# Selective scan: normed rows scaled by VectorE in place of ScalarE

## The chip, the cores and the metric

The kernel runs on one core of a Trainium2 chip, as one launch. The metric is the device time of an execution in microseconds (us), as the median of several executions. The engines are named as the profile names them: PE is TensorE (PEld its weight loads), DVE is VectorE, ACT is ScalarE, POOL is GpSimd, SP is SyncE. They run beside each other, each through its own instructions in a fixed order, and wait for one another by semaphores.

## What is computed

Four transformer layers on 32 sequences of 256 rows with 128 features, in fp32. Each layer normalises its rows, applies an attention-like part, adds it, normalises again and applies a feed-forward part. Only the first half of layer 0 bears on the change:

```python
h = _layernorm(x) * (1 + ca) + sa            # first norm, with per-sequence scale and shift
x = x + ga * attn(h)                         # attn: the part below

def attn(h):                                 # in outline
    n = _layernorm(h) * ln_w + ln_b          # second norm
    p = n @ proj_W.T + proj_b ; z = silu(p)
    for br in (forward, backward):
        u = softplus(p @ conv_W[br].T + conv_b[br])
        dbc = u @ deltaBC_W.T                # delta (64), B (16), C (16)
        delta = softplus(dbc[:, :64] @ dt_W.T + dt_b)
        # per feature d and state n (16 states), along the 256 rows of a sequence:
        #   hs[t] = exp(delta[t] * A[d, n]) * hs[t-1] + delta[t] * u[t] * B[t, n]
        #   y[t]  = sum over n of hs[t] * C[t, n] ; y += u * D
    return (y_forward + y_backward) * z + h

def _layernorm(x):
    return (x - mean(x)) / sqrt(var(x) + 1e-5)   # over the 128 features of a row
```

## The kernel before

The 8192 rows are cut into 16 batches of 512 (two sequences). `x[b]` stays in SBUF with features on partitions and rows along the free axis. The eight half layers run as eight stages, one after another; the change lies in the first, `scan_layer`.

A batch of the scan has 2 branches x 16 states = 32 recurrences along 512 rows. They are taken in 8 groups of four states, p = 8b to 8b + 7. For a group:

- PE multiplies `duT` with `Bd` into the PSUM tile `dB` (16 products of 32 rows; the tile has one buffer). `Bd` is the B of a branch spread out into a diagonal, made by POOL in four multiplications (`scan_b`, line 916).
- DVE runs four scans (`TENSOR_TENSOR_SCAN hs<-decay,dB`, line 953), one for each state, with the factors `decay` that ACT has made by Exp (`scan_decay`; a ring of 10 buffers).
- PE transposes the result in two halves into `hT` (one buffer), ACT copies each to `hsT`, and PE multiplies these with `Cd` into `y`, which collects the whole batch.

The scan of a group may start when its `dB` is complete, and the next `dB` may be written when the last of the four scans has read this one. The instructions are recorded in an order written out by hand: an agenda of steps, two for each group (2p and 2p + 1); PE, DVE, ACT and POOL keep that order. A batch has T = 16b as its first step, and what prepares batch b is put at steps before T, so it runs among the scans of batches b - 1 to b - 3; what prepares the first ones runs ahead of the first scan.

Each batch needs two norms (n = 1, starting at step o = T - 44, from `x`; n = 2, at o = T - 36, from `h`). A norm goes through these steps:

- o: `norm_rows`: four PE transposes give rows on partitions; ACT copies them from PSUM to `ln_xn` (four tiles of 128 rows, 128x512 together, one buffer).
- o + 1: `norm_sums`: DVE takes mean and variance (four `bn_stats` to `ln_st`, four `bn_aggr` to `ln_mv`); POOL adds the eps (`ln_v`).
- o + 2: `scan_roots`: ACT makes exp(-0.5 ln v) (`ln_t`, `ln_rs`); POOL refines it by a Newton step in four small instructions (`norm_newton`, lines 527 to 530, the last one writing `ln_rs`) and makes the shift -mean * root in two more (`ln_m`).
- o + 3, behind the work of that step: `norm_scale`: ACT scales `ln_xn` in place, four instructions of 128x128 with scale `ln_rs` and bias `ln_m`.
- o + 4: `norm_out`: PE transposes the four tiles back, ACT applies the factor and shift of the features (`h` or `xn`).

Of the eight groups of a batch, the fourth (p % 8 == 3) is the one whose odd step holds a scaling for n = 1, and the last (p % 8 == 7) that for n = 2. In the order of DVE the place after these steps' work lies between the four scans of that group and the four of the next. On POOL the newton steps are followed directly by the four `Bd` multiplications of a branch, at both places. `Bd` waits for ACT's copy `bc` (line 912).

The instructions of `norm_scale` have line 428 in the profile, where `act` records them; most of the others have line 320, of a wrapper that keeps the order, so the tiles' names tell them apart. PE's are at 416 (products) and 425 (transposes).

Of the kernel before, what the change touches and what calls it, by code (L numbers as in the profile page):

```python
# [25 lines left out]
ALU = mybir.AluOpType  # L26
# [312 lines left out]
class Program:  # L339
# [372 lines left out]
    def scan_layer(self, w):  # L712
# [7 lines left out]
        with ExitStack() as ctx:  # L720
# [14 lines left out]
            for n in range(10):  # L735
                t = self.wk_pool.tile([P, 2, SEQ], F, name=f"decay{n}", bufs=1)
# [6 lines left out]
            def put(t, f, *args):  # L743
                agenda.setdefault(t, []).append((f, args))
# [11 lines left out]
            behind, scale = {}, {}  # L756
# [7 lines left out]
            for b in range(NB):  # L764
                a = s[b] = {"b": b}
                T = 16 * b
                put(T, self.clear_regions)


                for o, n, src in ((T - 44, 1, lambda a: self.x[a["b"]]), (T - 36, 2, lambda a: a["h"])):  # L770

                    put(o, lambda a, n=n, src=src: a.update({("rows", n): self.norm_rows(src(a), sums=False)}), a)
                    put(o + 1, lambda a, n=n: a.update({("st", n): self.norm_sums(a["rows", n], nc.gpsimd)}), a)
                    put(o + 2, lambda a, n=n: self.scan_roots(a, n), a)
                    scale.setdefault(o + 3, []).append(lambda a=a, n=n: self.norm_scale(a["st", n][0], *a["r", n]))
                put(T - 40, self.scan_norm_out, a)
                put(T - 32, self.scan_norm_out2, s, a)
                put(T - 21, self.scan_proj, s, a)
                put(T - 20, self.scan_gate, s, a)
                put(T - 19, self.scan_gate2, s, a)  # L780
                for br in (0, 1):
                    o = T + 8 * br
                    put(T - 19 + 6 * br, self.scan_u, s, a, br)
                    put(T - 18 + 6 * br, self.scan_u2, s, a, br)
                    put(o - 15, self.scan_delta, s, a, br)
                    put(o - 14, self.scan_rows, s, a, br)
                    put(o - 13, self.scan_chunks, s, a)
                    put(o - 10, self.scan_turn, s, a, br)
                    put(o - 9, self.scan_b, s, a, br)
                    put(o - 5, self.scan_c, s, a, br)  # L790
                put(T - 4, lambda a: nc.gpsimd.tensor_scalar(a["uu"], a["uu"], w.vec[:, 6:7], None, ALU.mult), a)
                put(T + 21, self.scan_end, s, a)

                put(T + 25, lambda a: self.residual(0, 0, a["b"], a["y"]), a)
# [10 lines left out]

    def scan_roots(self, a, n):
        _, mv, v = a["st", n]
        a["r", n] = self.norm_newton(mv, v, self.norm_roots(v))

    def scan_norm_out(self, a):  # L810
        a["h"] = self.norm_out(a["st", 1][0], self.ada_mods(0, 0, a["b"]), "h")
# [2515 lines left out]
```

## Time and profile before

| | |
|---|---|
| time, median of 5 runs (lowest to highest) | 5791.92 us (5789.57 to 5795.16) |
| the profiled execution: its time, its span | 5801.96 us, 5800.2 us |
| mean granted TensorE clock of it | 0.952 |
| share of the span that is busy: PE, DVE, ACT, POOL | 90%, 67%, 63%, 51% |
| first to last scan (all 16 batches) | 120.2 us to 970.4 us of the span |
| scalings of `ln_xn` by ACT at line 428 | 128 instructions, 486 ns median, 23.8 us to 825.3 us |
| the same scaling done by DVE elsewhere in the program, SBUF to SBUF | 120 instructions, 329 / 345 / 793 ns (least, median, most) |
| four of them together | 1.11 us to 2.06 us |
| one `Bd` multiplication on POOL | 1048 ns (1043 to 1057) |

How to read it. The profile is of one execution, which took 10.04 us longer than the median of the runs. A line of the timeline begins with the start and the time from the first start to the last end (us from the start of the span), then engine, line, operation, out<-in with shapes, and how many equal instructions were merged (xN); in brackets stands the idle time of the engine before them and what ended it. Consecutive instructions on an engine overlap a little, so the next one can start before the shown end of the last. A line of the windows gives a stretch and its length, then the busy us and number of instructions of each engine, the clock granted to PE, and the share of the DMA engines.

### The profile page before, as it was taken

To read this page: it belongs to the slowest core of one execution; us is meant where nothing else is said; L and a number is where in the kernel's file an instruction comes from. 1 tells how busy PE (TensorE), PEld (TensorE's weight loads), DVE (VectorE), ACT (ScalarE), POOL (GpSimd) and SP (SyncE) were. 2 spreads that over 40 slices of the span, in tenths; PEclk is the share of its full clock that TensorE was granted. 3 is DMA by queue.
4 is the path that set the end of the run, shared out by engine and by line. 5 is a ranking of instruction groups with operands and counts; after the bars stand their busy time and mean duration, and the time that the engine had idled before them with its cause. 6 is when DMAs were issued, how large, how long until landed. Compare 5 with 4: busy or idle time off the path is not lost. (4 is left out here: it accounts for less than half of the span.)

```text
span 5800.2 us, 159517 instructions
## 1 busy us (share of the span) xinstructions
PE 5238.8 (90%) x66753; PEld 2967.5 (51%) x66753; DVE 3894.2 (67%) x7981; ACT 3643.6 (63%) x5550; POOL 2969.8 (51%) x3597
## 2 busy tenths in 40 slices
PE   5888887879989999999999877999899998999976
PEld 3666665446646666665666443555322222545543
DVE  3888887631156766666665645888778763677778
ACT  4999996223355555555555644666588885777733
POOL 3666663566457777776766334665455552111100
PEclk8999998789999999999999887999999997999988
DMA  2111101124312222222222221110244441000010
GB/s 74 45 36 48 47 34 45 37 73 135 103 53 74 75 74 74 74 74 77 76 71 72 84 37 40 37 34 27 62 97 98 98 97 32 20 23 23 21 41 28
DMA packets 311313, 343.48 MB, mean 59 GB/s; under 512 B 106624, under 2 KB 206208, under 8 KB 310336
## 3 DMA queue, kind: packets, MB, share of 16 engines
q1 hardware_dynamic: 269456, 240.04, 14.9%
q0 software_dynamic: 23920, 58.05, 3.9%
q10 hardware_dynamic: 17216, 35.19, 1.6%
q8 instruction: 524, 8.59, 0.6%
q14 instruction: 197, 1.61, 0.1%
HBM read 139.17 MB, written 122.68 MB: 45 GB/s over the span
## 5 line engine op out<-in xcount | busy, mean ns | idle before, releaser
L320 POOL TENSOR_SCALAR_AFFINE_SELECT E<-E 128x512 f32<-128x512 f32 (+2 forms) x1024 | 795.2, 779 | 674.1 <-ACT E L320 649.9
L320 DVE TENSOR_REDUCE mt<-S 128x4 f32<-128x1024 f32 (+2 forms) x768 | 756.1, 999 | 419.0 <-PE S L416 415.3
L320 ACT ACTIVATE E<-S 128x1024 f32<-128x1024 f32 (+2 forms) x704 | 632.0, 907 | 528.2 <-PE S L416 484.6
L320 DVE TENSOR_TENSOR_SCAN hs<-decay,dB 128x512 f32<-128x512 f32 x512 | 582.9, 1205 | 103.8 <-PE dB L416 81.5
L428 ACT ACTIVATE hid<-S,bigw 128x1024 f32<-128x1024 f32 x512 | 537.9, 1113 | 86.1 <-PE S L416 80.4
L320 DVE TENSOR_TENSOR E<-S,cst 128x1024 f32<-128x1024 f32 x320 | 390.1, 1219 | 195.7 <-PE S L416 182.7
L416 PE MATMUL S<-kx,q 32*128 32x512 f32 (+1 forms) x2048 | 519.6, 598 | 1.9 <-DVE mt L320 1.5
L416 PE MATMUL S<-qa,kx 32*128 32x256 f32 x4096 | 511.3, 372 | 10.6 <-ACT E L320 5.2
L2871 POOL TENSOR_TENSOR acc<-acc,ye 128x512 f32<-128x512 f32 x256 | 346.2, 1352 | 336.6 <-DVE ye L320 324.7
L320 ACT COPY E<-S 128x1024 f32<-128x1024 f32 x320 | 324.3, 1014 | 281.7 <-PE S L416 252.2
L416 PEld LDWEIGHTS S<-qa,kx 32*128 32x128 f32 x4096 | 326.8, 185 | 172.6 <-issue 67.5
L416 PE MATMUL S<-qG,f 32*128 32x512 f32 x2560 | 365.0, 640 | 12.1 <-DVE E L320 12.1
L416 PE MATMUL S<-hm,bigw 32*128 32x512 f32 x2048 | 352.9, 649 | 9.5 <-ACT hid L428 8.3
L428 ACT ACTIVATE decay<-dl,A 128x510 f32<-128x510 f32 x512 | 338.7, 713 | 0.0
L425 PE MATMUL hT<-cst,hs 128*128 128x128 f32 x2048 | 279.6, 280 | 29.5 <-ACT hsT L428 22.7
L428 ACT ACTIVATE hsT<-hT 128x1024 f32<-128x1024 f32 x256 | 260.1, 1016 | 58.2 <-PE hT L425 56.1
L416 PE MATMUL po<-E,vz 128*32 128x256 f32 x4096 | 286.7, 363 | 1.4 <-POOL E L320 1.4
L416 PE MATMUL po<-E,vzl 128*32 128x128 f32 x8192 | 284.9, 274 | 1.3 <-POOL E L320 1.0
L416 PE MATMUL tp<-hid,bigw 128*32 128x512 f32 x2048 | 275.2, 610 | 8.2 <-DVE ye L320 6.9
L416 PE MATMUL tp<-h,w 128*32 128x256 f32 (+1 forms) x2592 | 258.7, 465 | 21.3 <-ACT kx L320 10.0
L416 PEld LDWEIGHTS po<-E,vzl 128*32 128x32 f32 x8192 | 225.0, 110 | 103.3 <-ACT phi_e L320 45.5
L320 DVE TENSOR_TENSOR ye<-tp,gb 128x512 f32<-128x512 f32 x256 | 174.2, 685 | 147.3 <-issue 78.2
(557 smaller groups left out, 11949.2 us busy)
## 6 DMA issues: line engine op xcount, KB each, us to landing
gb<-gT SPq DMA_DIRECT2D x256, 256.0 KB
wide<-oc SPq DMA_DIRECT2D x192, 256.0 KB
regions<-zeros ACTq DMA_DIRECT2D x16, 2048.0 KB
nm<-wide SPq DMA_DIRECT2D x384, 64.0 KB
rb<-far SPq DMA_DIRECT2D x384, 64.0 KB
rx<-far SPq DMA_DIRECT2D x64, 256.0 KB
expert_rows<-eo SPq DMA_DIRECT2D x39, 256.0 KB
bigw<-in_s SPq DMA_DIRECT2D x18, 256.0 KB
```

Of the source, the lines that this page charges most:

```text
L320: made = self.tc.keep_in_program_order(op(*args, **kw))
L416: return self.tc.keep_in_program_order(self.nc.tensor.matmul(out, lhsT, rhs, start=start, stop=stop, **kw))
L425: return self.tc.keep_in_program_order(self.nc.tensor.transpose(out, in_, self.c.ident[:k, :k]))
L428: ins = self.nc.scalar.activation(*args, **kw)
L2871: nc.gpsimd.tensor_tensor(a["acc"], a["acc"], ye, ALU.add)
```

## The change

The four scalings of a norm in the scan stage are recorded for DVE in place of ACT, at the same point of the program: `tensor_scalar` with two operations, subtract the mean, multiply by the root, in place on `ln_xn`. The shift is no longer made, so two small POOL instructions of each norm go. The 16 x 2 norms of the stage are all changed; the other stages are not.

```diff
-                    scale.setdefault(o + 3, []).append(lambda a=a, n=n: self.norm_scale(a["st", n][0], *a["r", n]))
+                    scale.setdefault(o + 3, []).append(lambda a=a, n=n: self.scan_norm_scale(a, n))
...
     def scan_roots(self, a, n):
         _, mv, v = a["st", n]
-        a["r", n] = self.norm_newton(mv, v, self.norm_roots(v))
+        a["r", n], _ = self.norm_newton(mv, v, self.norm_roots(v), False)
+
+    def scan_norm_scale(self, a, n):
+        xn, mv, _ = a["st", n]
+        for t in range(4):
+            self.nc.vector.tensor_scalar(
+                xn[:, t], xn[:, t], mv[:, t, 0:1], a["r", n][:, t : t + 1], ALU.subtract, ALU.mult
+            )
```

In the order of the built programs, ACT has 128 instructions less, POOL 64 less and DVE 128 more; all else stands in the same order on every engine.

## Prediction

> **What bounds it now.** I read the windows by batch first, then the timeline of one steady batch engine by engine (715.10 us to 769.04 us), then every place where DVE does this scaling already.
>
> The windows of two batches of the scan: one with both norms, and the next, which holds nearly no norm work.
>
> ```profile
> core 0: us, PE busy (x) PEld busy (x) DVE busy (x) ACT busy (x) POOL busy (x), PEclk, DMA share, GB/s
> 769.03:822.96 53.93, 47.83 (x700) 33.81 (x700) 46.05 (x60) 51.41 (x86) 35.54 (x44) 1.00 0.12 43
> 822.96:874.84 51.88, 45.17 (x688) 32.35 (x688) 44.22 (x44) 47.55 (x74) 33.03 (x31) 1.00 0.13 45
> ```
>
> A batch takes 53.93 us and ACT is busy for 51.41 of them: the fullest engine, but not alone. Without nearly all norm work the next batch takes 51.88, only 2.05 less though ACT has 3.86 less to do. So the period is a chain through PE, DVE and ACT, and must be followed.
>
> DVE's timeline:
>
> ```profile
> 720.51 0.75 DVE L320 TENSOR_SCALAR dl<-tp,w 128x512 f32<-128x512 f32 x1 [0.86 <-PE tp L416]
> 735.85 4.56 DVE L320 TENSOR_TENSOR_SCAN hs<-decay,dB 128x512 f32<-128x512 f32 x4
> 741.76 4.55 DVE L320 TENSOR_TENSOR_SCAN hs<-decay,dB 128x512 f32<-128x512 f32 x4 [1.36 <-PE dB L416]
> 760.70 0.75 DVE L320 TENSOR_SCALAR u<-tp,w 128x512 f32<-128x512 f32 x1 [0.87 <-PE tp L416]
> 769.04 1.22 DVE L320 TENSOR_TENSOR_SCAN hs<-decay,dB 128x512 f32<-128x512 f32 x1 [1.36 <-PE dB L416]
> ```
>
> At both places of the new scaling (ahead of 741.76 and of 769.04) DVE idles 1.36 us while PE refills `dB`. Four scalings alone take 1.11, so they would fit, if their root is ready and nothing stands in their way. ACT, POOL and PE there:
>
> ```profile
> 740.71 0.26 ACT L428 ACTIVATE bc<-tp 128x128 f32<-128x128 f32 x1
> 742.09 1.65 ACT L428 ACTIVATE ln_xn<-ln_xn,ln_m,ln_rs 128x128 f32<-128x128 f32 x4
> 749.54 1.03 ACT L428 ACTIVATE hsT<-hT 128x1024 f32<-128x1024 f32 x1 [0.64 <-PE hT L425]
> 768.48 0.26 ACT L428 ACTIVATE bc<-tp 128x128 f32<-128x128 f32 x1
> ```
>
> ```profile
> 739.61 0.20 POOL L320 TENSOR_TENSOR ln_rs<-ln_rs,ln_t 128x4 f32<-128x4 f32 x1
> 741.05 4.07 POOL L320 TENSOR_TENSOR Bd<-cst,bc 128x512 f32<-128x512 f32 x4 [0.65 <-ACT bc L428]
> 768.27 0.20 POOL L320 TENSOR_TENSOR ln_rs<-ln_rs,ln_t 128x4 f32<-128x4 f32 x1
> ```
>
> ```profile
> 742.63 1.48 PE L425 MATMUL tp<-cst,ln_xn 128*128 128x128 f32 x4
> 747.25 1.17 PE L416 MATMUL dB<-Bd,duT 32*128 32x128 f32 x32
> ```
>
> POOL starts `Bd`, four pieces of 1.05 us, just when DVE will scale. How the two get on is seen in another stage (merged rows share a start; x2 and x3 are the first two and three of the x4):
>
> ```profile
> 4301.09 1.11 DVE L320 TENSOR_SCALAR ln_xn<-ln_xn,ln_mv,ln_rs 128x128 f32<-128x128 f32 x4
> ...
> 1706.43 2.06 DVE L320 TENSOR_SCALAR ln_xn<-ln_xn,ln_mv,ln_rs 128x128 f32<-128x128 f32 x4
> 1706.43 1.10 DVE L320 TENSOR_SCALAR ln_xn<-ln_xn,ln_mv,ln_rs 128x128 f32<-128x128 f32 x2
> 1706.43 1.81 DVE L320 TENSOR_SCALAR ln_xn<-ln_xn,ln_mv,ln_rs 128x128 f32<-128x128 f32 x3
> 1707.05 0.41 POOL L320 TENSOR_SCALAR_AFFINE_SELECT E<-E 128x256 f32<-128x256 f32 x1
> 1707.43 0.73 POOL L320 TENSOR_TENSOR glob<-glob,lv 128x256 f32<-128x256 f32 x1
> ```
>
> Alone, pieces follow each other by 0.26 and the last ends 0.34 after its start. Beside POOL the second ended at 1707.53, 0.07 after the select's end (1707.46), the third at 1708.24, 0.08 after `glob`'s end (1708.16). I read: a piece needs something it shares with POOL from 0.26 to 0.34 after its start; if a POOL instruction is in it, the piece waits for that one's end, slips through in 0.08, and the next piece meets the next POOL instruction.
>
> When POOL takes it is seen in the same stage:
>
> ```profile
> 758.24 2.50 POOL L320 TENSOR_TENSOR Cd<-cst,bc 128x512 f32<-128x512 f32 x2
> 759.03 0.81 DVE L320 SCALAR_TENSOR_TENSOR sg<-xp,sg 128x512 f32<-128x512 f32 x1
> ```
>
> The second `Cd` starts 1.01 after the first, 759.25, and ends at 760.74: 1.49 instead of 1.05, held for 0.44 until `sg` ended at 759.84. So it wanted the thing about 0.15 after its start.
>
> **The change, part by part.** Removed from ACT: 8 scalings a batch, 2 x 1.54 us of its queue (742.09 to the next start at 743.63). Removed from POOL: two `ln_m` instructions a norm, 0.6 us, so that `Bd` can follow `ln_rs` sooner. Added to DVE: 8 pieces a batch, and a wait for POOL's `ln_rs`; behind it in DVE's queue stand the next four scans.
>
> *Middle scaling.* `ln_rs` is ready at 739.81, the scan of the fourth group ends at 740.4. The pieces start at about 740.33 and want the shared thing at 740.59, 740.85, 741.11 and 741.37. `Bd` starts at 741.05 and wants it at 741.20: three pieces pass, the fourth waits for the first `Bd`, until 742.10. The scans start at 742.10 instead of 741.76: 0.34 lost. What is won: PE's transposes were paced by ACT and ended at 744.11; now all is there when PE comes to them (742.65), and four take 0.60. PE is ready for `dB` at about 746.3 instead of 747.25, but the scans end at 746.24 + 0.34, so `dB` starts at 746.60: 0.65 earlier. ACT, which idled 0.64 at 749.54 for the `hT` behind this `dB`, goes on 0.65 earlier, and works without a gap to the second norm's roots; so all of that comes 0.65 earlier, POOL's newton and `bc` too (the wait of 0.87 at 760.70 shrinks with it).
>
> *Late scaling.* The root is ready at 768.47 - 0.65 = 767.82. The first piece starts at 767.86 and wants the shared thing at 768.12. `bc` ends at 768.09, `Bd` starts 0.08 behind it as before (740.97 to 741.05), 768.17, and wants it at 768.32. One piece passes; the second wants it at 768.38, and from there each waits for one more `Bd`: ends at 769.22, 770.23 and 771.24, and 771.31 for the last piece. The next batch's scans start at 771.24 instead of 769.04: 2.20 lost. Given back: before, the next `dB` came 5.88 us after the scans' start (715.10 to 720.98), since PE was late behind the paced transposes (the wait of 0.86 at 720.51). Now PE has its transposes, products and `hT` done by 774.8 (771.4 plus 0.65, 1.09, 1.02, 0.64), and `dB` starts right behind the scans, 4.48 after their start (741.76 to 746.24): 1.40 won. Net 0.80 lost per batch. From that `dB` on the order of waits is the old one (ACT waits for `hT`, PE for `yT`), so it repeats: 13 of the 16 batches hold both scalings (26 of 32), 13 x 0.80 = 10.4 us lost.
>
> *Ahead of the first scan* lie six scalings in a nearly serial chain. In the first, `ln_rs` ends at 23.20 and ACT scaled from 23.83 to 25.48; DVE alone ends at 24.35, 1.13 won; four such, 4.5 won. At the fifth (`ln_rs` 96.12, `bc` 96.07) `Bd` is free to start at about 96.32 (it came 0.20 behind POOL's last small instruction before), and three pieces wait: 99.47 instead of 98.39, 1.1 lost. At the sixth (122.21) `Bd` can follow the newton at once, so all four wait, to 126.3; and the first scan, which ran from 120.24, stands behind them: the second `dB` comes at 130.75 instead of 128.05, 2.7 lost. Together 0.7 won.
>
> Sum: +10.4 - 0.7 = +9.7 us. The profiled execution would go from 5801.96 to 5811.7; it lies 10.04 over the median, which goes from 5791.92 to 5801.6. Stages run one after another, so I take the shift as passed on whole.
>
> The Trainium skill has a rule on the shared thing (SBUF — State Buffer, section "SBUF: two separate sides"): VectorE in a two-port mode and GpSimd share a port pair as an exclusive lock, held by whichever starts first for the whole instruction, which speaks against this change. Taken by starts, it would let the second late piece go ahead of `Bd`, one wait less and a sum of about -3.4 us. The row decides against that: the second piece at 1706.98 had started before the select at 1707.05 and still ended behind it.
>
> **The rivals.**
> 1. No collision (faster). `Bd`'s small broadcast inputs, or its place, keep it out of DVE's way. Then the middle scaling costs nothing and `dB` and the roots come 0.95 earlier; the late one ends at 768.71, the scans start 0.42 earlier and the `dB` behind them 0.42 + 1.40 = 1.82. 13 x 1.82 + 5.9 ahead of the scans = 29.6 won: 5762. For it: no row shows `Bd` itself against this scaling. Against: `Cd`, made alike, held and was held. 0.17.
> 2. One more piece waits (slower): the late first piece (0.20 ahead of `Bd`) or the middle third (0.09 ahead) misses its place. Each costs one more `Bd`, 1.01 a batch: 13 us more, 5814.7; both 5828. It decides where the root comes that much later or `bc` earlier. 0.23, and 0.03 of it for both.
> 3. One piece less waits: 1.01 less a batch, 5788.5. 0.08.
>
> **How the numbers follow.** The forecast has 0.52; its own range, some 0.45 us a batch either way, is 5796 to 5808. The range leaves out rival 1 and both misses (0.20): 5786 to 5818. No change is within 0.2%, 11.6 us, about what a measurement of this kernel can tell: up to 5803.5. A third of the forecast lies above: slower 0.18 + 0.23 = 0.41, faster 0.17, same 0.42.
>
> **What would show it.** In the profile after: four scalings of about 1.8 us in the middle place and 3.4 in the late one, the last pieces ending 0.08 behind a `Bd`; no wait for `tp` before `dl`; ACT under 49 us busy in a batch of 54.7. Scalings of 1.1 us in both places, or a batch under 53, prove me wrong, and so would `Bd` pieces that grow instead.

## The result and the profile after

The kernel after the change takes 5806.85 us in the median of its runs, the kernel before 5792.18 in the runs beside them: a ratio of 1.0025 (95% interval 1.0020 to 1.0031), 14.7 us slower. The prediction was 5801.6, 9.7 slower.

The profiled execution of after has a span of 5800.9 us, against 5800.2 of before, and would hide this. In it the program behind the scan happened to run quicker: PE was busy for 5211.3 us (5238.8 before), at a mean clock of 0.955 (0.952). Inside the scan, where PE's clock is 1.00 in both profiles from 133 us on, but for two stretches of 3.4 us in after (taken up with the prediction below), the two can be compared: the last group's scans start at 965.85 us before and at 980.65 after, 14.8 later. That is about the 14.7 of the medians (whose interval is 11.6 to 18.0 us), so the scan is where to look. Its steady batch (columns as in the windows of before):

```profile
728.67:783.64 54.97, 46.53 (x698) 33.69 (x698) 51.22 (x70) 48.69 (x77) 34.75 (x40) 1.00 0.12 42
```

The batch takes 54.97 us instead of 53.93. ACT, the fullest engine before, now works 48.69 of it instead of 51.41. DVE's 46.05 have become 51.22: 5.17 more, where eight pieces (a piece is one scaling of 128x128) alone, 1.11 for four, would have added 2.2. DVE's timeline shows where the rest is, first the late place, then the middle one:

```profile
725.30 3.44 DVE L320 TENSOR_SCALAR ln_xn<-ln_xn,ln_mv,ln_rs 128x128 f32<-128x128 f32 x4 [0.77 <-POOL ln_rs L320]
728.67 4.54 DVE L320 TENSOR_TENSOR_SCAN hs<-decay,dB 128x512 f32<-128x512 f32 x4
733.13 0.72 DVE L320 TENSOR_SCALAR dl<-tp,w 128x512 f32<-128x512 f32 x1
752.61 1.86 DVE L320 TENSOR_SCALAR ln_xn<-ln_xn,ln_mv,ln_rs 128x128 f32<-128x128 f32 x4
754.40 4.54 DVE L320 TENSOR_TENSOR_SCAN hs<-decay,dB 128x512 f32<-128x512 f32 x4
```

Four scalings take 3.44 us late and 1.86 in the middle. The wait for `tp` before `dl` (0.86 at 720.51 before) is gone. POOL at the two places:

```profile
725.61 4.06 POOL L320 TENSOR_TENSOR Bd<-cst,bc 128x512 f32<-128x512 f32 x4 [0.34 <-ACT bc L428]
753.35 4.07 POOL L320 TENSOR_TENSOR Bd<-cst,bc 128x512 f32<-128x512 f32 x4 [1.25 <-ACT bc L428]
```

`Bd` loses nothing: 4.07 before, 4.06 and 4.07 now. DVE pays the whole collision. The two groups of pieces, cut off after the second (late) and after the third (middle):

```profile
725.30 1.44 DVE L320 TENSOR_SCALAR ln_xn<-ln_xn,ln_mv,ln_rs 128x128 f32<-128x128 f32 x2 [0.77 <-POOL ln_rs L320]
752.61 0.84 DVE L320 TENSOR_SCALAR ln_xn<-ln_xn,ln_mv,ln_rs 128x128 f32<-128x128 f32 x3
```

Late, the second piece ends at 726.74, and the first `Bd` at 726.66. The third and fourth end 1.00 and 2.00 later, each behind one more `Bd`. In the middle three pieces pass in 0.84, and only the fourth waits: it starts at 753.36 and ends at 754.48, 0.08 behind the first `Bd`'s end at 754.40. PE's refills of `dB` behind the two groups of scans:

```profile
728.80 0.33 PE L425 MATMUL tp<-cst,ln_xn 128*128 128x128 f32 x1 [0.68 <-DVE ln_xn L320]
...
733.27 1.17 PE L416 MATMUL dB<-Bd,duT 32*128 32x128 f32 x32 [1.10 <-DVE hs L320]
759.00 1.17 PE L416 MATMUL dB<-Bd,duT 32*128 32x128 f32 x32 [0.30 <-DVE hs L320]
```

PE had been late at both refills. Now it stands ready and waits for the scans (`<-DVE hs`): 1.10 and 0.30 us.

### The profile page after: what moved, and what is told of

It is laid out like the page before. It is cut to its first block, busy times and chain, and to the rows that moved or that the text cites. A ratio compares the mean times of both kernels' runs of the same rounds, so it can differ in the third digit from the quotient of the medians.

```text
span 5800.9 us, 159456 instructions
## 1 busy us (share of the span) xinstructions
PE 5211.3 (90%) x66753; PEld 2964.5 (51%) x66753; DVE 3968.3 (68%) x8109; ACT 3599.0 (62%) x5422; POOL 2957.4 (51%) x3533
```

## The experiments

Theory T1 is the prediction's: a piece that meets a `Bd` instruction waits for its end, one instruction for each piece; this is the loss, and what ACT is relieved of wins back a part. T2: the loss is DVE's added work in front of the scans and its wait for POOL's root, whatever lies beside it. T3: the two engines share a bandwidth in proportion. The experiments ran in two later series, each on one chip, in which the kernel before took 5724.61 us and 5728.03 us; each time stands beside the before of its own series. The period is that of a steady batch, and the last column but one is the start of the last group's scans.

| kernel | four scalings, middle / late | period | last scans start | time; ratio to before (interval) |
|---|---|---|---|---|
| before; before, second series | (ACT) | 53.93; 53.94 | 965.85; 966.57 | |
| after | 1.86 / 3.44 | 54.97 | 980.65 | 5806.85; 1.0025 (1.0020 to 1.0031) |
| middle only | 1.86 / (ACT) | 53.42 | 957.40 | 5725.35; 1.0001 (0.9992 to 1.0010) |
| middle only, second series | 1.86 / (ACT) | 53.42 | 958.76 | 5719.03; 0.9983 (0.9974 to 0.9992) |
| late only | (ACT) / 3.44 | 55.50 | 987.46 | 5751.91; 1.0043 (1.0029 to 1.0057) |
| `Bd` in halves | 1.44 / 2.15 | 53.35 | 956.85 | 5713.07; 0.9981 (0.9972 to 0.9990) |
| `Bd` held | 1.09 / 1.11 | 52.32 | 942.10 | 5696.58; 0.9960 (0.9945 to 0.9975) |
| before, `Bd` held | (ACT) | 54.47 | 971.33 | 5727.38; 1.0001 (0.9992 to 1.0010) |
| `Bd` and `u` held | 1.09 / 1.10 | 51.90 | 933.73 | 5693.29; 0.9943 (0.9930 to 0.9957) |

**One place alone.** The condition on `n` is put around the recording of the scaling and of the root; the other norm is scaled by ACT as before.

```diff
-                    scale.setdefault(o + 3, []).append(lambda a=a, n=n: self.scan_norm_scale(a, n))
+                    if n == 1:        # "late only": n == 2
+                        scale.setdefault(o + 3, []).append(lambda a=a, n=n: self.scan_norm_scale(a, n))
+                    else:
+                        scale.setdefault(o + 3, []).append(lambda a=a, n=n: self.norm_scale(a["st", n][0], *a["r", n]))
```

> Only the scaling of the first norm of a batch (the middle place, after the fourth group) is done by VectorE; that of the second norm is ScalarE's again, with its shift. T1 (each late piece waits for one more Bd instruction on GpSimd's side; the middle place loses 0.34 us and wins back more through ScalarE): four in 1.86 us in the middle place as in the changed kernel, a batch period of about 53.4 us (53.93 before, 54.97 after), the end of the scan stage about 7 us earlier than before, time about 7 us under before. T2 (VectorE's added work in front of the scans is the loss, whatever lies beside it): half of the loss, a period of about 54.4 and about 7 us over before. T3 (VectorE and GpSimd share bandwidth in proportion): as T2, since both places hold four pieces beside a Bd.

> Only the scaling of the second norm (the late place, after the eighth group) is done by VectorE; that of the first norm is ScalarE's again, with its shift. T1: four in 3.4 us or, as nothing brings the roots forward now, up to one Bd more (4.1 us); a batch period of about 55.5 us (53.93 before, 54.97 after), more than with both changed, and about 20 us over before. T2 and T3: half of the loss, a period of about 54.4 and about 7 us over before.

The middle place alone wins 0.51 us a batch, the late one alone loses 1.57. Their sum, +1.06, is the +1.04 of the whole change: the effects of the two places add up, and all of the loss sits in the late one. T2 and T3 wanted half the loss from each, so they fail as they stand. Only the late place has a wait for POOL's root (0.77 us in after, 0.84 here); that the loss is this wait is not excluded by these two runs, and the runs with `Bd` held below settle it. The late pieces took 3.44 with no relief at the middle place, so the relief there is not what set their number of waits.

The middle version's time did not follow at first: its scan ended 8.4 us sooner than in the first profile of before, and its time was 0.7 us longer. It was run again beside a profile of the kernel before on the same chip.

> The kernel before, unchanged, profiled on the chip of these runs, so that its stages can be set beside those of the others: a batch period of 53.93 us and the last group of the scan starting 965.5 us into the span, as in the first profile (all theories).

> The version with only the middle scaling on VectorE once more, beside the kernel before on the same chip: its scan was 8.4 us shorter in the first profile, its time 0.7 us longer. If the scan's gain is passed on whole (T1), about 8 us under before; if something behind the scan takes it back, no change, and the stage behind the scan that is longer is to be seen beside the profile of the kernel before.

There it took 9.0 us less, its scan 7.8. From the start of the last group's scans to the end of the span the two profiled executions of this kernel took 4774.1 and 4758.2 us, and the executions of the kernel before alone lie between 5715.88 and 5733.82 us in the first series: what lies behind the scan differs by as much as is sought here. The ratios, 1.0001 and 0.9983, have intervals that just meet. These two series alone don't settle whether the scan's gain is passed on whole. The larger shifts agree with it, within intervals of 8 us or so either way: against 966.57 the scan ended 20.9 us later with the late place alone (27.3 in the time), 24.5 sooner with `Bd` held (28.0), 32.8 sooner in the fastest version (34.7).

**`Bd` in instructions of half the size.**

```diff
-        full = [P, 4, 32, 4]
+        full = [P, 2, 32, 4]
...
-            self.nc.gpsimd.tensor_tensor(
-                d[:, g::4],
...
+            for j in (0, 8):
+                self.nc.gpsimd.tensor_tensor(
+                    d[:, j + g : j + 8 : 4],
```

> The changed kernel, with each of the four Bd multiplications cut into two of half the size (8 in place of 4, the same elements, an estimated 0.53 to 0.6 us each). T1 (one GpSimd instruction for each piece): a piece now waits for half as much, so four take about 2.1 us in the late place (3.44 after) and about 1.45 in the middle one (1.86 after), and the period falls to about 53.4 us. T2: no change in the period, 54.97. T3 (a share of the bandwidth): the pieces take as long as before, 3.4 and 1.9 us, and the period stays at 54.97 or grows by the added instructions.

DVE, then POOL:

```profile
706.47 2.15 DVE L320 TENSOR_SCALAR ln_xn<-ln_xn,ln_mv,ln_rs 128x128 f32<-128x128 f32 x4 [0.75 <-POOL ln_rs L320]
732.49 1.44 DVE L320 TENSOR_SCALAR ln_xn<-ln_xn,ln_mv,ln_rs 128x128 f32<-128x128 f32 x4
```

```profile
706.78 4.63 POOL L320 TENSOR_TENSOR Bd<-cst,bc 128x256 f32<-128x256 f32 x8 [0.34 <-ACT bc L428]
```

This is the test that tells T1 from T3. `Bd` as a whole grew from 4.06 to 4.63 us, so POOL moves the same data over a longer time, and still DVE's late pieces fell from 3.44 to 2.15. They follow POOL's instructions, which now end every 0.57 us instead of every 1.00: three waits are 3 x 0.43 = 1.29 shorter, and 3.44 - 1.29 = 2.15. Cutting another engine's instructions in two made the changed kernel faster than before, 11.5 us under it.

**`Bd` held until the scaling is done.** It is recorded behind the scaling, and POOL first copies one column of the last scaled tile, so that it waits for DVE.

```diff
                 for f in scale.get(t, ()):
-                    f()
+                    xn = f()
+                    if s["held"]:
+                        nc.gpsimd.tensor_copy(wk("past", (P, 1)), xn[:, 3, 0:1])
+                for work in s["held"]:
+                    self.scan_spread(*work)     # the four Bd multiplications
+                s["held"].clear()
```

> The changed kernel, with the four Bd multiplications recorded behind the scaling and held on GpSimd by a copy of one column of the scaled rows, so that Bd starts when the four pieces are done. Everything else is the same work. T1: four in 1.11 us at both places and ahead of the first scan; the scans start about 2.3 us sooner in the late place; Bd, made a few us later, is not late for its dB; a period of about 52.3 us (54.97 after, 53.93 before), time about 27 us under before. T2: the pieces and the wait for GpSimd's root still stand in front of the scans, so a period of 54 to 55 us and a time at or over before. T3: as T1 in the pieces, but the period falls only by what the pieces lose, 1 to 2 us.

DVE and POOL:

```profile
719.78 1.09 DVE L320 TENSOR_SCALAR ln_xn<-ln_xn,ln_mv,ln_rs 128x128 f32<-128x128 f32 x4
...
747.13 1.11 DVE L320 TENSOR_SCALAR ln_xn<-ln_xn,ln_mv,ln_rs 128x128 f32<-128x128 f32 x4 [0.78 <-POOL ln_rs L320]
748.16 4.55 DVE L320 TENSOR_TENSOR_SCAN hs<-decay,dB 128x512 f32<-128x512 f32 x4
```

```profile
748.31 0.18 POOL L320 COPY past<-ln_xn 128x1 f32<-128x1 f32 x1 [1.21 <-DVE ln_xn L320]
748.45 4.06 POOL L320 TENSOR_TENSOR Bd<-cst,bc 128x512 f32<-128x512 f32 x4
```

The same work in another order: four pieces in 1.1 us at both places, `Bd` as long as ever but later, a period of 52.32 (52.3 was expected), and 28.0 us under before (27). DVE still waits 0.78 for POOL's root in the late place, so this wait was not the main loss. The collision is worth 2.65 us a batch, and without it the change does what its words suggest.

**The same hold in the kernel before**, where ACT scales.

> The kernel before (ScalarE scales), with Bd held on GpSimd until the scaling is done, in the same way. T1: nothing to win, since ScalarE's scaling shares nothing with GpSimd: 1.64 us for four as before, a period of 53.9 us, no change in time (within 0.2%). If the time of Bd itself is what the held version wins by, the period falls to about 52.3 here too.

Here I was wrong about the period: 54.47, not 53.9. `Bd` starts when ACT's scaling is done, 2.9 us later against the scans, and there it meets another piece of DVE's work, the residual `x`. DVE in the kernel before (second series), then in this one, then POOL in this one:

```profile
746.95 0.86 DVE L320 SCALAR_TENSOR_TENSOR x<-y,mods,x 128x256 f32<-128x256 f32 x2
```

```profile
750.64 2.23 DVE L320 SCALAR_TENSOR_TENSOR x<-y,mods,x 128x256 f32<-128x256 f32 x2
```

```profile
748.35 4.24 POOL L320 TENSOR_TENSOR Bd<-cst,bc 128x512 f32<-128x512 f32 x4
```

Two operations of 0.86 together took 2.23, and this time `Bd` paid too, 4.24 for 4.06. So holding `Bd` is no gain by itself, and the collision is not peculiar to the scaling: where `Bd` lands decides whom it hits. The scan ended 4.8 us later; the time, 0.6 us less with an interval of some 5 us either way, can't show that.

**`Bd` and `u` held.** What is left in the late place is DVE's wait of 0.78 for POOL's root, ahead of which POOL makes the 1.28 us addition of `u`. Here that addition goes behind the scaling too, ahead of `Bd`.

```diff
     def scan_u2(self, s, a, br):
-        self.soft_end(*a["soft"])
+        ...                              # ACT's two steps as before
+        if br: add()                     # GpSimd's u <- sp_m + u
+        else: s["next"] = add            # recorded at the next step, behind the scaling
```

> The kernel with Bd held behind the scaling, and the addition that makes u for the forward branch (1.28 us on GpSimd, ahead of the late Newton step so far) held behind the scaling too, ahead of Bd, so that the root comes sooner. T1: the late root, 0.78 us late so far, comes before the eighth group's scans end; four in 1.1 us in both places without a wait; the scans start behind the refill of dB alone, 0.4 us sooner; a period of about 51.9 us (52.32 with Bd held alone), time about 5 us under that one and about 33 us under before. If the wait for GpSimd's root is not what holds the scans there, the period stays at 52.3.

```profile
738.76 1.10 DVE L320 TENSOR_SCALAR ln_xn<-ln_xn,ln_mv,ln_rs 128x128 f32<-128x128 f32 x4
740.21 4.56 DVE L320 TENSOR_TENSOR_SCAN hs<-decay,dB 128x512 f32<-128x512 f32 x4 [0.35 <-PE dB L416]
```

DVE now waits for no root, its four pieces lie inside the refill of `dB`, and the scans wait 0.35 for that refill alone. The period is 51.90, as expected, and the time 34.7 us under before (33 expected): the fastest version here. T2 had this much of the truth: the wait for the root was worth 0.42 us a batch.

## Why the prediction was right, and what it sized wrong

Direction, place and mechanism held. The pieces took 1.86 and 3.44 us; the prediction's own steps give 742.18 - 740.33 = 1.85 and 771.31 - 767.86 = 3.45. One piece waits in the middle, three late, none ahead of the first scan at the first four scalings (1.11 each, as forecast). The transposes are no longer paced by ACT, and `dl` no longer waits. ACT is busy for 48.69 of the batch ("under 49"), and `Bd` did not grow. Rival 1's premise, that `Bd` keeps out of DVE's way, was wrong, though the run without the collision gave the gain that rival priced (28.0 against 29.6). Rivals 2 and 3 asked for one wait more or less, and at both places of a batch the count was exact. By the prediction's own line for no change (up to 5803.5) the result is slower, to which it gave 0.41, a hair less than the 0.42 for no change.

The weighing of the Trainium skill's rule (SBUF — State Buffer, section "SBUF: two separate sides") also came out as the prediction had it: the second late piece started at 725.57, ahead of `Bd` at 725.61, and yet ended behind it. Still, neither this row nor the one the prediction relied on is decisive. The start that the profile shows for a piece lies about 0.08 ahead of the end of the piece before it; counted from that end (725.65 here, 1707.06 there), POOL was first, as the rule wants. A row of another stage decides, in which DVE's previous operation had ended 0.03 us earlier. DVE, then POOL, in after:

```profile
3583.78 0.76 DVE L320 TENSOR_SCALAR ln_v<-ln_mv 128x4 f32<-128x4 f32 x1
3583.88 0.63 POOL L320 TENSOR_SCALAR_AFFINE_SELECT E<-E 128x512 f32<-128x512 f32 x1
```

This operation takes 0.17 us in the median of its 79 runs there. Here it started 0.10 ahead of the select and still ended 0.03 behind the select's end, at 3584.54; the same stands in the profiles of the middle place alone and of `Bd` in halves (0.76 us each). Whoever starts first does not simply hold the port here. That the one which comes to need it first gets it is the reading that fits all these rows.

What the forecast's 9.7 lacks of the scan's 14.8 is 5.1 us:

- *The time from a group's scans to the next `dB`* was taken as 4.48 us, the distance to DVE's next start (741.76 to 746.24). But DVE's instructions overlap a little, and PE waits for the real end: 728.67 to 733.27 and 754.40 to 759.00 are 4.60. The trace of before has it wherever PE waits for `hs`. It enters twice: the gain behind the late scaling is 0.12 smaller, and the `dB` behind the middle one comes 0.54 earlier, not 0.65, so the late root does too. The net loss is 1.04 a batch instead of 0.80, 2.9 us over twelve batches.
- *Ahead of the first scan* four pieces met a `Bd` at the fifth scaling, not three (4.13 us instead of an expected 3.3): `Bd` followed POOL's last small instruction by 0.03, not by the 0.20 taken over from before. The gain of 0.7 was one of 0.1: the second group of the first batch starts at 129.96 instead of 130.06.
- *The first batch* lost 1.94 instead of 0.80 (from its second group to the same group of the next). In two profiles of the kernel before it took 52.54 and 53.34 us, so a good part may be chance. PE's clock may be part of it. At the start of the scan it is 0.50, and it rises to 1.00 at different times: 0.5 us ahead of the second group's scans in the shorter of these two, 1.4 us behind their start in the longer, 3.1 us behind it in after. How much of the 1.94 this makes is not shown.
- *Irregular batches*: two of after's batches took 0.45 more each, and those of before came to 0.3 together. Net, 0.6. Each of the two holds 3.4 us of half clock; here is the first, the batch and then the stretch in it:

```profile
294.35:349.77 55.42, 48.10 (x700) 34.56 (x700) 51.22 (x69) 48.80 (x77) 34.76 (x39) 0.97 0.12 42
344.70:348.10 3.40, 3.40 (x18) 1.88 (x20) 3.40 (x4) 3.12 (x6) 0.00 (x0) 0.50 1.03 384
```

  The transfers that fill the DMA engines there (1.03) are not the reason: the batch before has such a stretch too (289.00 to 292.40), at a clock of 1.00, and takes 54.97. With the late place alone, two batches of 55.95 and 55.96 instead of 55.50 hold such a stretch each. So 0.9 of the 14.8 goes with the clock of this execution, not with the change.

The steps add up: -0.1 ahead, +1.9 in the first batch, +13.0 in the next twelve, none where there are no norms, 14.8 in all. The stated range allowed for one `Bd` more or less, 13 us, and held the result easily; the forecast's own range, 5796 to 5808, held it with 1.15 us to spare, since all four misses went the same way.

## What to carry to other kernels

An idle gap on an engine is not free to fill: read what its neighbour on the same memory does in that very microsecond, and count instructions that meet, not their bytes. Where two engines collide instruction by instruction, the remedy is an order, so that the short critical work goes first and the long work with slack waits, and it must be looked at again where the displaced work lands. And take "when is it done" from the row of whoever waits for it, not from the next start on the same engine.

## What was not expected of the hardware

Who pays for a collision is not settled by the pair of operations. A scaling of 128x128 waited for whole `Bd` instructions and cost them nothing (1.04 us each, with or without). The residual's operations of 128x256 waited too, and also made `Bd` longer, by 0.18 us over four. With `Cd` and `sg` it goes either way. In the kernel before (second series) `sg` came to it first: it took 0.82, and the four `Cd` 4.52. In the same kernel with `Bd` held, `sg` started 0.36 behind the fourth `Cd`, and it was `sg` that waited. POOL, then DVE, there:

```profile
761.17 4.06 POOL L320 TENSOR_TENSOR Cd<-cst,bc 128x512 f32<-128x512 f32 x4
764.56 1.23 DVE L320 SCALAR_TENSOR_TENSOR sg<-xp,sg 128x512 f32<-128x512 f32 x1
```

The operation that waited ended 0.08 (scaling), 0.28 (`x`) and 0.56 (`sg`) behind the POOL instruction it had waited for. If this is how long each still needs the shared thing, as the prediction read it for the scaling, the next POOL instruction, which wants it about 0.15 after its start, meets only the longer two; that fits these rows and was not tested further. The scans, which ran beside `Bd` as well, kept their 4.54 us.

And the smaller instructions that helped DVE cost POOL 14%: 4.63 us for eight halves against 4.06 for four wholes.
